# Cross-attention on one core: the key products A by eleven 64x64 block products instead of twelve, in a rewritten order of steps

## The chip, the cores and the metric

The kernel runs on one core of a Trainium2 chip, as one program. The metric is the device time of one execution in microseconds (us); the time before is the median of three executions. The engines are TensorE (PE; its weight loads are PEld), VectorE (DVE), ScalarE (ACT), GpSimd (POOL) and SyncE (SP, which issues transfers).

## The reference

Cross-attention of 16 batches, 256 queries of 256 features against 77 keys of 192 features, 8 heads of width 256, with a residual and a layer norm. The mask that is given is all ones.

```python
Q = (x @ Wq).reshape(B, -1, H, D).transpose(0, 2, 1, 3)      # x: 16 x 256 x 256
K = (ctx @ Wk).reshape(B, -1, H, D).transpose(0, 2, 1, 3)    # ctx: 16 x 77 x 192
V = (ctx @ Wv).reshape(B, -1, H, D).transpose(0, 2, 1, 3)
score = einsum('bhqd,bhkd->bhqk', Q, K) / sqrt(D)            # H = 8, D = 256
attn = softmax(where(mask, score, -inf), axis=-1)
o = einsum('bhqk,bhkd->bqhd', attn, V).reshape(B, -1, H * D)
out = o @ Wo + x
out = (out - mean(out)) * rsqrt(var(out) + 1e-5) * gamma + beta
```

All is float32.

## The kernel before

**What is computed.** Weights are multiplied first: G = Wq Wk^T / 16 for each head (tile `gA` holds the first 128 of ctx's 192 features, `gB` the last 64), and U = Wv Wo (`uA`, `uB`). Then A = G^T ctx^T for each head gives "keys" that x meets directly: scores = x A. A is made for a group of four batches at a time, `prepare_a`, into the tile `a`: for a pair of heads, 128-row products by `gA` (L193) and 64-row products by `gB` (L205), both in tiles of 32 output rows, 308 columns (4 batches x 77 keys); group 3 is made two batches at a time for its last pairs. ctx U ("values" that already passed Wo) comes from `prepare_vw` (L227 and L238), tile `vw`. 

**One batch** has two tiles of 128 queries. For each tile: `scores` (L303, PE), `shift` (L320, DVE: adds the mask's bias and finds each row's maximum), `exponential` (L340, ACT, eight instructions, one a head), a reciprocal (L355, DVE) and `weigh` (L361, POOL: multiplies by the reciprocal), `turn` (L371, DVE: transposes into `pT`). Then attention times values is done for both tiles together by `seven(b)` (L450, PE: seven block products instead of eight), which needs `sums(b)` (L431 to L434, POOL: sums of blocks of pT) and `differences(b)` (L414, POOL: sums of blocks of vw, tile `ts`). `add_seven(b)` puts the products together: `add_product` on DVE (L498: x plus the products in PSUM) and five additions on POOL (L484). Last the layer norm of each tile: `finish` (L506 and L509, DVE: statistics), `spread` (L527 and L528, ACT: logarithm and exponential that give the reciprocal deviation `rstd`), `normalise` (L548 and L577, DVE), and a transfer out.

**Order.** Nothing is planned by a scheduler: each engine runs its instructions in the order in which the program's text issues them, and waits on semaphores. The text is one loop over b from -1 to 14 whose body does the scores of batch b+1, its softmax, `seven(b)`, and the layer norm of batch b-1; every second body also makes the values of two batches and two pairs of heads of a coming A. A batch pair (a turn) is thus one body with that work and one without. Results of matmuls go through eight PSUM banks, given out in rotation (tag "mm"): a product that takes a bank waits until what was in it eight allocations ago has been read. ACT's copies (L963) empty the banks of vw and A. The work ahead of the loop (transposes, G, U, group 0 of A, the first softmax) is the prologue.

## Time and profile before

| | |
|---|---|
| median of 3 executions | 270.27 us (270.22 to 270.64) |
| the profiled execution | 269.95 us |
| its span in the trace | 268.2 us |
| granted clock of TensorE | 1.0 |
| busy PE / DVE / ACT / POOL | 262.5 / 185.9 / 157.6 / 173.2 us |

Busy times are sums over the span. A row of the timeline gives start, length, engine, line, operation, output and inputs, shape and how many in a row; a group's row gives count, total busy time and the mean of one in ns, then the idle time in front of it and what ended that. The engine's idle time counts only where the chain that ends last passes through it. The granted clock is 1.0 when TensorE runs at its full rate.

### The profile page before, as it was taken

How to read it: one execution, taken by the hardware profiler on the slowest of the kernel's cores; microseconds unless marked ns; L12 is line 12 of the kernel's file. 1: busy time of each engine (PE TensorE's matmuls, PEld its weight loads, DVE VectorE, ACT ScalarE, POOL GpSimd, SP SyncE). 2: the span in 40 equal slices, each digit the busy share in tenths (PEclk: the TensorE clock that was granted, in tenths of full speed). 3: DMA queues.
4: the chain of work that ended last, by engine and by line, in shares of the span. 5: the costliest groups of instructions: out<-in, count | busy, mean ns of one | idle time of the engine just before them, and what ended most of it. 6: DMA issues, size and time to landing. Idle time of an engine off the chain costs nothing.

```text
span 268.2 us, 14455 instructions
## 1 busy us (share of the span) xinstructions
PE 262.5 (98%) x6090; PEld 191.8 (72%) x6090; DVE 185.9 (69%) x808; ACT 157.6 (59%) x667; POOL 173.2 (65%) x240
## 2 busy tenths in 40 slices
PE   8999999999999999999999999999999999999992
PEld 8566578944984699459944995499669957985662
DVE  1555967493583868665886379647977887799785
ACT  3243336536857565955596468737775595636772
POOL 1042005728399739994799669965998799585452
PEclk9999999999999999999999999999999999999999
DMA  6989987901500130232012401340034010100112
GB/s 190 217 199 228 334 138 142 311 21 34 129 7 2 46 80 2 63 111 71 5 43 90 112 5 43 91 113 2 6 120 122 4 45 2 44 22 22 46 40 80
DMA packets 41696, 22.69 MB, mean 85 GB/s; under 512 B 24144, under 2 KB 40608, under 8 KB 41632
## 3 DMA queue, kind: packets, MB, share of 16 engines
q1 hardware_dynamic: 41248, 20.98, 30.1%
q0 software_dynamic: 384, 0.79, 1.3%
q8 instruction: 48, 0.79, 1.3%
q14 instruction: 16, 0.13, 0.2%
HBM read 17.57 MB, written 4.19 MB: 81 GB/s over the span
## 4 chain that ended last, share of the span: by engine, by line
PE 98%; DVE 1%; issue 0%; DVEq 0%
PE ps L303 25%; PE pa L193 13%; PE pv L227 11%; PE po L450 11%; PE pm L450 8%; PE pa L205 6%; PE pv L238 6%; PE po L383 4%; PE pu L773 3%; PE pr L263 2%; PE pgb L834 2%; PE pw L787 1%; PE idle L703 1%; PE pr L274 1%; PE phb L850 1%; PE po L399 1%
## 5 line engine op out<-in xcount | busy, mean ns | idle before, releaser
L340 ACT ACTIVATE s<-s,top 128x77 f32<-128x77 f32 x256 | 85.3, 346 | 44.2 <-DVE top L320 37.9
L303 PE MATMUL ps<-a,xT 128*32 128x154 f32 x2048 | 69.9, 294 | 0.0
L303 PEld LDWEIGHTS ps<-a,xT 128*32 128x32 f32 x2048 | 66.2, 110 | 1.2 <-issue 0.4
L361 POOL TENSOR_TENSOR p<-s,rden 128x512 f32<-128x512 f32 x64 | 47.5, 768 | 29.5 <-DVE rden L355 29.4
L320 DVE CUSTOM_DVE_ANT_0 s<-ps,bias 128x77 f32<-128x77 f32 x256 | 43.5, 232 | 14.3 <-PE ps L303 14.3
L340 ACT ACTIVATION_READ_ACCUMULATOR s<-s,top 128x1 f32 x224 | 42.0, 187 | 0.0
L193 PE MATMUL pa<-cA,gA 128*32 128x308 f32 (+1 forms) x576 | 36.6, 395 | 0.0
L193 PEld LDWEIGHTS pa<-cA,gA 128*32 128x32 f32 x576 | 18.3, 110 | 21.0 <-issue 7.0
L484 POOL TENSOR_TENSOR xg<-xg,m 128x256 f32<-128x256 f32 x39 | 28.7, 736 | 6.6 <-DVE xg L498 4.5
L577 DVE SCALAR_TENSOR_TENSOR xg<-xg,rstd,bet 128x256 f32<-128x256 f32 x27 | 22.9, 847 | 14.0 <-ACT rstd L528 12.6
L227 PE MATMUL pv<-uA,cA 128*32 128x512 f32 x256 | 30.6, 595 | 0.0
L371 DVE STREAM_TRANSPOSE pT<-p 128x640 f32<-128x640 f32 x32 | 25.5, 821 | 3.4 <-POOL p L361 3.3
L414 POOL TENSOR_TENSOR ts<-vw 128x768 f32<-128x768 f32 x13 | 24.0, 1848 | 5.9 <-ACT vw L963 5.9
L963 ACT COPY vw<-pv 128x512 f32<-128x512 f32 x32 | 17.8, 584 | 14.8 <-PE pv L227 8.3
L498 DVE TENSOR_TENSOR xg<-po,xg 128x256 f32<-128x256 f32 x31 | 11.5, 405 | 13.8 <-PE po L450 13.3
L320 DVE DVE_READ_ACCUMULATOR2_ANT top<- 128x1 f32 x256 | 20.8, 81 | 0.0
L205 PE MATMUL pa<-cB,gB 64*32 64x308 f32 (+2 forms) x512 | 20.4, 387 | 0.0
L963 ACT COPY a<-pa 128x308 f32<-128x308 f32 (+1 forms) x56 | 18.9, 395 | 1.9 <-PE pa L193 0.4
L205 PEld LDWEIGHTS pa<-cB,gB 64*32 64x32 f32 (+1 forms) x512 | 11.0, 110 | 11.4 <-issue 6.2
L548 DVE SCALAR_TENSOR_TENSOR xg<-xg,mv,gam 128x256 f32<-128x256 f32 x30 | 17.6, 588 | 0.1
L238 PE MATMUL pv<-uB,cB 64*32 64x512 f32 x256 | 17.3, 597 | 0.0
L227 PEld LDWEIGHTS pv<-uA,cA 128*32 128x32 f32 x256 | 7.5, 109 | 12.8 <-issue 9.9
(119 smaller groups left out, 404.1 us busy)
## 6 DMA issues: line engine op xcount, KB each, us to landing
xg<-in_x_dram SPq DMA_DIRECT2D x8, 512.0 KB, 4.4
xT<-in_x_dram SPq DMA_DIRECT2D x56, 64.0 KB, 2.6
out_dram<-xg SPq DMA_DIRECT2D x11, 256.0 KB, 2.2
wo<-in_L_xattn_Wo_dram SPq DMA_DIRECT2D x4, 512.0 KB, 7.8
wq_blk<-in_L_xattn_Wq_dram SPq DMA_DIRECT2D x12, 128.0 KB, 4.3
out_dram<-xg SPq DMA_DIRECT2D x10, 128.0 KB, 1.9
wk_blk<-in_L_xattn_Wk_dram SPq DMA_DIRECT2D x12, 96.0 KB, 3.6
wvT<-in_L_xattn_Wv_dram POOLq DMA_DIRECT2D x8, 96.0 KB, 6.6
```

Of the source, the lines that this page charges most:

```text
L193: nc.tensor.matmul(flat(o[i * BK : (i + 1) * BK]), gA[:, h, cols(dc, i)], flat(cA[:, batches, :]), start=not rest_first and n in opening, ...
L205: nc.tensor.matmul(flat(banks[j + k][i * BK : (i + wide) * BK]), gB[half(k), h // 2, dc * P + i * BK : dc * P + (i + wide) * BK], flat(cB[ ...
L227: nc.tensor.matmul(pv[k][i * BK : (i + 1) * BK], cA[:, b, k * BK : (k + 1) * BK], uA[:, parts, :, i], start=not rest_first, stop=rest_first,)
L238: nc.tensor.matmul(pv[k][i * BK : (i + 1) * BK], cB[half(k), b, k * BK : (k + 1) * BK], uB[half(k), parts, :, i], start=rest_first, stop=n ...
L303: nc.tensor.matmul(ps[m // 2][i * BK : (i + 1) * BK, m % 2 * 2 * S2 : (m % 2 + 1) * 2 * S2], xT_of[t // PT][:, j * NM + m, dc], flat(a_of[ ...
L320: nc.vector.tensor_tensor_reduce(s[:, h], ps[a][:, k * S2 : (k + 1) * S2], bias[:, b, :], scale=-1.0, scalar=FAR, op0=ALU.add, op1=ALU.min ...
L340: nc.scalar.activation(s[:, h], s[:, h], AF.Exp, bias=top[:, one], scale=-1.0, accum_out=den[:, one] if summed_by_act(t) else None,)
L361: nc.gpsimd.tensor_tensor(part, e_mh[:, :, :, keys], rden_mh.unsqueeze(3).to_broadcast(list(part.shape)), ALU.mult,)
L371: nc.vector.transpose(pT_of[t].rearrange("p n m q -> p m n q"), p.rearrange("p m (n k) -> p m n k", k=BK),)
L450: nc.tensor.matmul(out[i * BK : (i + 1) * BK], weight[:, i], moving, start=first and n == 0, stop=final and n == len(terms) - 1,)
L484: nc.gpsimd.tensor_tensor(to, to, what, ALU.add)
L963: nc.scalar.copy(dst, src)
```

## The change

**A by blocks.** For groups 1 to 3 and as long as b < 10, A of a pair of heads is made by `prepare_fast` instead of `prepare_a`. Each head's product is cut into blocks: eight block products of the first 128 features are replaced by seven (sums of blocks of G, tile `gS` and `gC`, times sums of blocks of ctx, tiles `cT` and `cD`), and four of the last 64 features stay, eleven in all. All are tiles of 64x64 with 154 columns (two batches x 77). Per pair of heads there are 44 matmuls (L360 in the kernel after). Two of a pair's 154-column results are copied by ACT (L369), and DVE puts the rest together with four additions a head (L372), each reading one PSUM bank and `a`. The sums of blocks are formed once in the prologue on POOL, with a few copies on ACT (`sums_of_g`, `last_sums_of_g`, `sums_of_c`, `differences_of_c`); `gA` is laid out by halves of the features for them.

**Statistics.** For the tiles of batches 0 to 9, `finish` takes the mean and the variance by two ACT activations that accumulate (L681, L682) instead of two DVE instructions.

**Order.** The loop's first ten bodies are replaced by pairs of a `long_step` (with the values and two pairs of A) and a `short_step`; the old body, a little simplified, does the rest. The layer norm of a batch comes later than before.

The core of the diff:

```diff
+        def products():
...
+            for pair in pairs():
...
+                for i in range(2):
+                    for ((bank, n), weight, moving), (start, stop, _) in zip(pair, flags):
+                        nc.tensor.matmul(
+                            bank[half(i), n],
+                            weight(i),
+                            moving,
+                            start=start,
+                            stop=stop,
+                        )
+                for ((bank, n), _, _), (_, _, one) in zip(pair, flags):
+                    if one:
+                        nc.scalar.copy(blocks[lone[id(bank)]][:, 0], by_batch(bank)[:, n])
...
+        def put_together(e):
+            mid, end, of = by_batch(mids[e]), by_batch(ends[e]), blocks[e]
+            plus(of[:, 3], mid[:, 2], of[:, 0])
+            plus(of[:, 1:3], mid[:, 0:2], of[:, 3:4].to_broadcast([P, 2, HB, S2]))
+            plus(of[:, 3], mid[:, 0], of[:, 2])
+            plus(of[:, 0:3], end, of[:, 0:3])
...
+        if by_act(t):
+            junk = st.tile([P, DI], F32, tag="junk", name=f"junk_{t}", bufs=1)
+            mean, var = (mv_of[g][:, j, n : n + 1] for n in range(2))
+            nc.scalar.activation(junk, y, AF.Identity, scale=1.0 / DI, accum_out=mean)
+            nc.scalar.activation(junk, y, AF.Square, bias=mean, scale=-1.0, accum_out=var)
+            return
         bn = st.tile([P, 6], F32, tag="bn", name=f"bn_{t}")
         nc.vector.bn_stats(bn, y)
...
+        turn_rest_last()
+        sums_of_c(1, 2)
         sum_of(uB)
         for t in range(QT):
             exponential(t)
             weigh(t)
+        differences_of_c(1, NG)
+        sums_of_c(2, NG)
...
+    def long_step(b):
...
+        statistics(tiles_of(b - 2))
+        works = work_of(b + 1) + work_of(b + 2)
+        for part_A, *_ in works:
+            part_A()
+        if now:
+            seven(b)
+        for _, part_B, _ in works:
+            part_B()
...
+            fasts.append(prepare_fast(g, n + k))
...
+        statistics(tiles_of(b - 1))
...
+        for t in tiles_of(b - 2):
+            normalise(t)
+        turn_some_x(g, n)
...
+        fasts[0][1](0)
+        fasts[0][1](1)
+        fasts[1][1](0)
+        behind.append(partial(fasts[1][1], 1))
+        for t in tiles_of(b - 1):
+            behind.append(partial(normalise, t))
...
+    def short_step(b):
...
+        seven(b)
+        weigh(new[0])
+        for _ in range(2):
+            if behind:
+                behind.pop(0)()
...
+        weigh(new[1])
+        turn(new[0])
+        while behind:
+            behind.pop(0)()
+        turn(new[1])
+        sums(b + 1)
+        add_seven(b)
...
+    ready = B - GB - GB // 2 - 1
+    for b in range(-1, ready, 2):
+        long_step(b)
+        short_step(b + 1)
+    statistics(tiles_of(ready - 2))
-    for b in range(-1, B - 1):
+    for b in range(ready, B - 1):
```

**POOL, the short step of a turn.** `ts` are the differences, `m` and `xg` the additions of `add_seven`, `ss` the sums, `pT` the turned tiles. Before:

```order
L414 TENSOR_TENSOR ts_1667<-vw_1378 128x768 [waits PE_49]
L484 TENSOR_TENSOR m_1735<-m_1735 128x128 [waits Activation_49]
L484 TENSOR_TENSOR m_1735<-m_1735 128x128 [waits Pool_49]
L484 TENSOR_TENSOR xg_518<-xg_518,m_1735 128x256 [waits DMAHW7_49,DVE_49]
L484 TENSOR_TENSOR xg_518<-xg_518,m_1735 128x2x128 [waits DVE_49,Pool_49]
L484 TENSOR_TENSOR xg_518<-xg_518,m_1735 128x256 [waits Pool_49]
L431 TENSOR_TENSOR ss_1750<-pT_1741 128x256
L432 TENSOR_TENSOR ss_1750<-pT_1741,pT_1739 128x256
L433 TENSOR_TENSOR ss_1750<-pT_1741,ss_1750 128x256 [waits Pool_49]
L434 TENSOR_TENSOR ss_1750<-pT_1739,ss_1750 128x256 [waits Pool_49]
```

After, the same step:

```order
L602 TENSOR_TENSOR ss_1838<-pT_1836 128x256 [waits DVE_49]
L603 TENSOR_TENSOR ss_1838<-pT_1836,pT_1831 128x256
L604 TENSOR_TENSOR ss_1838<-pT_1836,ss_1838 128x256 [waits Pool_49]
L605 TENSOR_TENSOR ss_1838<-pT_1831,ss_1838 128x256 [waits Pool_49]
L655 TENSOR_TENSOR m_1814<-m_1814 128x128 [waits Activation_49]
L655 TENSOR_TENSOR m_1814<-m_1814 128x128 [waits Pool_49]
L655 TENSOR_TENSOR xg_532<-xg_532,m_1814 128x256 [waits DMAHW7_49,DVE_49]
L655 TENSOR_TENSOR xg_532<-xg_532,m_1814 128x2x128 [waits DVE_49,Pool_49]
L655 TENSOR_TENSOR xg_532<-xg_532,m_1814 128x256 [waits Pool_49]
L532 TENSOR_TENSOR p_88<-s_1918,rden_2188 128x4x128 [waits DVE_49]
```

The four sums stand ahead of the five additions, the differences have gone to the long step, and the next long step's weighing (`p`) follows behind the additions.

**DVE, the short step, behind the shift.** `bn` and `mv` are statistics, `rden` the reciprocal, `xg` the rows that are normalised. Before:

```order
L506 BN_STATS bn_2482<-xg_831 128x6 [waits Pool_49]
L509 BN_AGGR mv_2484<-bn_2482 128x2 [waits DVE_49]
L355 RECIPROCAL rden_2486<-den_2473 128x8 [waits Activation_49]
L506 BN_STATS bn_2499<-xg_831 128x6 [waits Pool_49]
L509 BN_AGGR mv_2484<-bn_2499 128x2 [waits DVE_49]
L355 RECIPROCAL rden_2502<-den_2490 128x8 [waits Activation_49]
L548 SCALAR_TENSOR_TENSOR xg_831<-xg_831,mv_2484,gam 128x256
L577 SCALAR_TENSOR_TENSOR xg_831<-xg_831,rstd_2513,bet 128x256 [waits DVE_49,Activation_49]
L371 STREAM_TRANSPOSE pT_2655<-p_85 128x4x5x32 [waits Pool_49]
L371 STREAM_TRANSPOSE pT_2657<-p_86 128x4x5x32 [waits Pool_49]
```

After (`a` from `pf` are the additions that put A together):

```order
L526 RECIPROCAL rden_3026<-den_2940 128x8 [waits Activation_49]
L372 TENSOR_TENSOR a_2073<-pf_7_1_2734,a_2073 128x2x77
L372 TENSOR_TENSOR a_2073<-pf_7_1_2734,a_2073 128x4x77 [waits DVE_49]
L372 TENSOR_TENSOR a_2073<-pf_7_1_2734,a_2073 128x2x77 [waits DVE_49]
L372 TENSOR_TENSOR a_2073<-pf_7_1_2735,a_2073 128x6x77 [waits DVE_49]
L725 SCALAR_TENSOR_TENSOR xg_1033<-xg_1033,mv_2782,gam 128x256
L754 SCALAR_TENSOR_TENSOR xg_1033<-xg_1033,rstd_2790,bet 128x256 [waits DVE_49]
L526 RECIPROCAL rden_3036<-den_2949 128x8 [waits Activation_49]
L542 STREAM_TRANSPOSE pT_3040<-p_88 128x4x5x32 [waits Pool_49]
L725 SCALAR_TENSOR_TENSOR xg_1033<-xg_1033,mv_2782,gam 128x256
L754 SCALAR_TENSOR_TENSOR xg_1033<-xg_1033,rstd_2790,bet 128x256 [waits DVE_49]
L542 STREAM_TRANSPOSE pT_3045<-p_89 128x4x5x32 [waits Pool_49]
```

The statistics have left; the fourth head's additions and the normalisations of two tiles stand between the reciprocals and the turned tiles.

**ACT at batch 9**, where the paired steps end; `vw` and `a` are the copies that empty banks. Before:

```order
L340 ACTIVATE s_3537,den_3622<-s_3537,top_3538 128x77 [waits DVE_49,Pool_49]
L340 ACTIVATE s_3537,den_3622<-s_3537,top_3538 128x77 [waits DVE_49] x7
L963 COPY vw_3552<-pv_0_3553 128x4x128 [waits PE_49]
L963 COPY vw_3552<-pv_1_3554 128x4x128 [waits PE_49]
L963 COPY a_2988<-pa_4_0_0_3555 128x2x77 [waits PE_49]
L963 COPY a_2988<-pa_5_0_0_3556 128x2x77 [waits PE_49]
L963 COPY a_2988<-pa_4_0_0_3555 128x2x77
```

After:

```order
L511 ACTIVATE s_3740,den_3820<-s_3740,top_3741 128x77 [waits DVE_49,Pool_49]
L511 ACTIVATE s_3740,den_3820<-s_3740,top_3741 128x77 [waits DVE_49] x7
L681 ACTIVATE junk_3830,mv_3829<-xg_2223 128x256 [waits DMAHW6_49,Pool_49]
L682 ACTIVATE junk_3830,mv_3829<-xg_2223,mv_3829 128x256 [waits Activation_49]
L511 ACTIVATE s_3750,den_3837<-s_3750,top_3751 128x77 [waits DVE_49] x8
L681 ACTIVATE junk_3846,mv_3829<-xg_2223 128x256 [waits Activation_49,Pool_49]
L682 ACTIVATE junk_3846,mv_3829<-xg_2223,mv_3829 128x256 [waits Activation_49]
L1145 COPY vw_3767<-pv_0_3768 128x4x128 [waits PE_49]
L1145 COPY vw_3767<-pv_1_3769 128x4x128 [waits PE_49]
```

The statistics of two tiles, which wait for POOL, stand between the exponentials and ahead of the copies.

More of the change, by code (lines that the diff above doesn't have):

```diff
@@ L216, in prepare_a, with parts_of_g, sums_of_g @@
         return part_A, part_B, copies
+    add, subtract = (
+        partial(nc.gpsimd.tensor_tensor, op=op) for op in (ALU.add, ALU.subtract)
+    )
+    def parts_of_g():
+        parts = gA.rearrange("p (u e) (dc i c) -> p dc e u i c", e=2, dc=2, c=BK)
+        sums = gS.rearrange("p n (u e) (i c) -> p n e u i c", e=2, c=BK)
+        return [(parts, sums, e, own, other) for e, own, other in ((0, high, low), (1, low, high))]
+    def sums_of_g():
+        for parts, sums, e, own, other in parts_of_g():
+            nc.scalar.copy(sums[own, 0, e], parts[other, 1, e])
+            nc.scalar.copy(gC[own], gB[other, :, P:])
+        for parts, sums, e, own, other in parts_of_g():
+            s1, s2, s3 = (sums[own, n, e] for n in range(3))
+            add(s1, s1, parts[own, 1, e])
+            subtract(s2, s1, parts[own, 0, e])
+            subtract(s3, parts[own, 0, e], parts[own, 1, e])
@@ L893 @@
             a_of_pairs(a, rest_first=True)
+        gS = const.tile([P, 3, H, P], F32, tag="gS", name="gS")
+        sums_of_g()
         load_x(0)
@@ L976, with tiles_of, statistics @@
     last = NT - 1
-    for b in range(-1, B - 1):
+    def tiles_of(b):
+        return range(b * QT, (b + 1) * QT) if b >= 0 else ()
+    def statistics(tiles):
+        for t in tiles:
+            finish(t)
+        if tiles:
+            spread(tiles[0], tiles[-1] + 1)
+            invert(tiles[0], tiles[-1] + 1)
+    def long_step(b):
+        now, new = tiles_of(b), tiles_of(b + 1)
+        g, n = (b + 1) // GB + 1, (b + 1) % GB
+        if now:
+            for t in new:
+                scores(t)
+            for t in new:
+                shift(t)
+            for t in new:
+                exponential(t)
+        for m in range(0, 2) if b < 0 else range(b + 2, min(b + 3, B // 2)):
+            turn_last(m)
+        statistics(tiles_of(b - 2))
+        works = work_of(b + 1) + work_of(b + 2)
+        for part_A, *_ in works:
+            part_A()
+        if now:
+            seven(b)
+        for _, part_B, _ in works:
+            part_B()
+        fasts = []
+        for k in range(2):
+            fasts.append(prepare_fast(g, n + k))
+            if k == 0:
+                copy_out(works[:1])
+            fasts[k][0]()
+            if k == 0:
+                copy_out(works[1:])
+        statistics(tiles_of(b - 1))
+        if now:
+            for t in new:
+                weigh(t)
+        for t in new:
+            turn(t)
+        if b < 0:
+            for t in range(QT, GT, 2):
+                transpose_x(t)
+            bias_of(GB, B)
+        sums(b + 1)
+        if now:
+            add_seven(b)
+        for k in range(2):
+            differences(b + 1 + k)
+        for t in tiles_of(b - 2):
+            normalise(t)
+        turn_some_x(g, n)
+        if g < NG:
+            load_x((g * GB + n) // 2)
+            for k in range(2):
+                load_xT(g * GT + (n + k) * QT, g * GT + (n + k + 1) * QT, after_pool=k == 0)
+        fasts[0][1](0)
[4 more added lines that the diff above has]
+            behind.append(partial(normalise, t))
@@ new lines, in short_step @@
+    def short_step(b):
+        new = tiles_of(b + 1)
+        for t in new:
+            scores(t)
+        for t in new:
+            shift(t)
+        for t in new:
+            exponential(t)
+        seven(b)
[3 more added lines that the diff above has]
+                behind.pop(0)()
+        for m in range(b + 2, min(b + 3, B // 2)):
+            turn_last(m)
+        weigh(new[1])
[3 more added lines that the diff above has]
+        turn(new[1])
+        sums(b + 1)
+        add_seven(b)
@@ L980 @@
         new = range((b + 1) * QT, (b + 2) * QT)
-        for t in new if b >= 0 else ():
+        for t in new:
             scores(t)
-        for t in new if b >= 0 else ():
+        for t in new:
             shift(t)
@@ L991 @@
             load_x((g * GB + n) // 2)
-        for m in range(0, 2) if b < 0 else range(b + 2, min(b + 3, B // 2)):
-            turn_last(m)
         alone = b + 1 >= B - GB // 2
-        works = work_of(b + 1) if alone or n % 2 == 0 else []
-        for part_A, _, _ in works:
+        ahead = not alone and n % 2 == 0
+        works = work_of(b + 1) if alone or ahead else []
+        for part_A, *_ in works:
             part_A()
@@ L1017 @@
             break
-        for i, t in enumerate(new if b >= 0 else ()):
+        for i, t in enumerate(new):
             exponential(t)
-            if old:
-                finish(old[i])
+            finish(old[i])
             weigh(t)
-        ahead = works and not alone
-        if old and not ahead:
-            spread(old[0], old[-1] + 1)
         if ahead:
             copy_out(works)
-            if old:
-                spread(old[0], old[-1] + 1)
+        spread(old[0], old[-1] + 1)
+        if ahead:
             works = work_of(b + 2, rest_first=True)
@@ L1032 @@
                 part_B()
-            for part_A, _, _ in works:
+            for part_A, *_ in works:
                 part_A()
@@ L1040 @@
         if b < NS:
-            if now:
-                seven(b)
-            if old:
-                invert(old[0], old[-1] + 1)
-                normalise(old[0])
+            seven(b)
+            invert(old[0], old[-1] + 1)
+            normalise(old[0])
             for t in new:
                 turn(t)
-            if b < 0:
-                for t in range(QT, GT, 2):
-                    transpose_x(t)
-                bias_of(GB, B)
             if alone or ahead:
```

127 lines of the change are left out of this document (114 added, 13 removed).

## The prediction

> **What bounds the kernel now.** I read the page's busy line and chain first, then each engine's share in stretches of two batches, then the order of instructions inside one such stretch.
>
> ```profile
> PE 262.5 (98%) x6090; PEld 191.8 (72%) x6090; DVE 185.9 (69%) x808; ACT 157.6 (59%) x667; POOL 173.2 (65%) x240
> PE 98%; DVE 1%; issue 0%; DVEq 0%
> POOL 1042005728399739994799669965998799585452
> ```
>
> TensorE is busy for 98% of the span, and 98% of the chain that ended last is TensorE: every other engine's work is hidden today. (The third line is POOL's busy tenths in 40 slices of 6.7 us.) The stretches (columns: start and end, length, then busy time and instructions of PE, its weight loads, DVE, ACT, POOL, the granted clock, the DMA share) say how well:
>
> ```profile
> 50.00:55.40 5.40, 5.40 (x48) 4.67 (x50) 2.20 (x5) 2.12 (x10) 5.32 (x7) 1.00 0.75 248
> 55.40:61.27 5.87, 5.87 (x104) 2.41 (x104) 5.76 (x10) 1.60 (x5) 0.00 (x0) 1.00 0.01 3
> 134.95:162.83 27.88, 27.88 (x708) 20.22 (x704) 19.10 (x96) 18.18 (x84) 22.53 (x30) 1.00 0.21 60
> ```
>
> The third stretch is one turn of the steady state, two batches in 27.88 us, with the granted clock at 1.00. TensorE has no gap. POOL has 22.5 of 27.9, DVE 19.1, ACT 18.2: slack of 5, 9 and 10 us in sum, which says nothing yet of chains that run through several of them. The second row shows POOL wholly idle for 5.87 us before the first turn. TensorE's own pieces in a turn (start, length, operation; the next row's start is the true end):
>
> ```profile
> 80.72 2.26 PE L193 MATMUL pa<-cA,gA 128*32 128x308 f32 x32
> 82.91 1.09 PE L238 MATMUL pv<-uB,cB 64*32 64x512 f32 x16
> 83.79 1.24 PE L205 MATMUL pa<-cB,gB 64*32 64x308 f32 x32
> 84.83 1.06 PE L238 MATMUL pv<-uB,cB 64*32 64x512 f32 x16
> ...
> 88.60 2.26 PE L193 MATMUL pa<-cA,gA 128*32 128x308 f32 x32
> 90.67 0.62 PE L450 MATMUL pm<-vw,pT 128*32 128x128 f32 x16
> ...
> 94.59 4.37 PE L303 MATMUL ps<-a,xT 128*32 128x154 f32 x128
> 98.78 0.62 PE L450 MATMUL pm<-vw,pT 128*32 128x128 f32 x16
> ```
>
> **1. TensorE's saving.** For A, a turn holds two pairs of heads. A pair costs 2.07 us in L193 (88.60 to 90.67) and 1.04 in L205 (83.79 to 84.83), so two cost 6.22. Where L193 is followed by a tile of another height it takes 2.19 (80.72 to 82.91), so a change of tile shape costs 0.12; today a turn has two, 0.24. The new products have 64x64 tiles, as large in cells as 128x32, and 154 columns like the scores: 128 records in 4.19 us (94.59 to 98.78), 32.7 ns each. Two pairs take 2 x 88 records (the trace shows two per matmul written), 5.76 us, and three changes of shape, 0.36. That is 6.12 against 6.46, -0.34 a turn. Five turns: -1.7. The bounds come from the 64x64 rows of the prologue:
>
> ```profile
> 19.30 1.10 PE L850 MATMUL phb<-qT,kT_all 64*64 64x128 f32 x32
> 20.23 1.91 PE L834 MATMUL pgb<-qT,kT_all 64*64 64x256 f32 x32
> 21.95 1.22 PE L205 MATMUL pa<-cB,gB 64*64 64x308 f32 x16
> L773 PEld LDWEIGHTS pu<-wo,wv_turned 64*64 64x64 f32 x128 | 5.2, 133 | 2.0 <-PE pa L193 0.5
> ```
>
> 256 columns take 53.8 ns a record (1.72 us for 32), so 154 take 32.3, and the saving is 2.1. If four loads in parallel at 133 ns each set the pace (33.3), it is 1.2. I keep 32.7, the row with the same number of columns.
>
> The Trainium skill, "TensorE: Matmul & The Clock Gate", section "LDWEIGHTS (loading the stationary operand)", has a rule that speaks against this change: a load takes as long as its columns, columns/1.2 in ns. By it a 64-column load takes 53 ns; if they came one by one, 176 would take 9.4 us, 3.6 more than in my sum, and with five turns of that and nothing else late the time would be near 287. The row L850 does not bear it out: 32 loads and 32 matmuls of 128 columns pass in 0.93 us, 29 ns a pair. It stays as a rival below.
>
> **2. POOL's new prologue.** Sums of gA's blocks and of ctx's blocks are formed on POOL: before the sum for uB 8 operations of 154 columns, behind the first weighing one of 462 and 8 of 308. Prices:
>
> ```profile
> 50.11 1.27 POOL L902 TENSOR_TENSOR uB<-uB 128x512 f32<-128x512 f32 x1
> ...
> 52.69 2.71 POOL L361 TENSOR_TENSOR p<-s,rden 128x512 f32<-128x512 f32 x4
> 61.27 1.83 POOL L414 TENSOR_TENSOR ts<-vw 128x768 f32<-128x768 f32 x1 [5.88 <-ACT vw L963]
> ...
> 65.36 0.73 POOL L431 TENSOR_TENSOR ss<-pT 128x256 f32<-128x256 f32 x1
> ...
> 67.68 0.73 POOL L434 TENSOR_TENSOR ss<-pT,ss 128x256 f32<-128x256 f32 x1
> 71.77 1.06 PE L450 MATMUL pm<-ts,ss 128*32 128x128 f32 x32
> ```
>
> Two-input operations run at about 2.5 to 2.9 ns a column (1.27 for 512, 0.73 for 256); I give the copies 0.3 for 154 and 0.45 for 308. That makes 3.4 + 1.2 + 5.4 = 10.0 us behind 50.1. Of these 5.9 fall in the idle stretch. The first product with ts starts at 71.77 now, at 71.4 with the shorter first stage. POOL's queue ahead of ts is 50.1 + 3.4 (ctx sums) + 2.6 (uB) + 2.7 (weigh) + 6.6 + 2.2 (bias) + 3.05 (sums of batch 0) + 1.83 (ts) = 72.5. So TensorE waits +1.2 (0 if copies and broadcast sums are cheaper by a tenth, 2.5 if dearer by as much). The new sums of gA, some 10 us of POOL, lie before 50.1; there POOL's first seven slices have 12 of 70 tenths, so I count nothing for them; ACT's few new copies go the same way.
>
> **3. A ring through DVE and POOL.** DVE gets four additions a head, of 154, 308, 154 and 462 columns, each with one operand in PSUM and each dependent on the one before. Rows for that, and for everything else that DVE does in a turn:
>
> ```profile
> L498 DVE TENSOR_TENSOR xg<-po,xg 128x256 f32<-128x256 f32 x31 | 11.5, 405 | 13.8 <-PE po L450 13.3 <-PE po L383 0.5
> L516 DVE TENSOR_TENSOR xg<-po,xg 128x128 f32<-128x128 f32 x2 | 0.6, 286 | 0.0
> 108.05 0.23 DVE L320 CUSTOM_DVE_ANT_0 s<-ps,bias 128x77 f32<-128x77 f32 x1
> 108.21 0.55 DVE L548 SCALAR_TENSOR_TENSOR xg<-xg,mv,gam 128x256 f32<-128x256 f32 x1
> 108.79 0.84 DVE L577 SCALAR_TENSOR_TENSOR xg<-xg,rstd,bet 128x256 f32<-128x256 f32 x1
> ...
> 115.35 1.56 DVE L371 STREAM_TRANSPOSE pT<-p 128x640 f32<-128x640 f32 x2
> 116.83 1.26 DVE L165 STREAM_TRANSPOSE xT<-xT 128x512 f32<-128x512 f32 x2
> ...
> 122.72 0.76 DVE L498 TENSOR_TENSOR xg<-po,xg 128x256 f32<-128x256 f32 x2 [3.38 <-PE po L450]
> ...
> 130.39 0.48 DVE L577 SCALAR_TENSOR_TENSOR xg<-xg,rstd,bet 128x256 f32<-128x256 f32 x1
> L506 DVE BATCH_NORM_STATS2 bn<-xg 128x6 f32<-128x256 f32 x31 | 12.3, 396 | 0.1
> L509 DVE BATCH_NORM_AGGREGATE mv<-bn 128x2 f32<-128x6 f32 x31 | 5.6, 182 | 1.1
> 77.41 0.99 POOL L484 TENSOR_TENSOR m<-m 128x128 f32<-128x128 f32 x2
> 78.36 2.36 POOL L484 TENSOR_TENSOR xg<-xg,m 128x256 f32<-128x256 f32 x3
> ```
>
> 405 for 256 columns and 286 for 128 make 0.93 ns a column and 167 fixed: 0.31 + 0.45 + 0.31 + 0.60 = 1.67, with releases 1.7 a head, 6.8 a turn. Against it go four tiles' statistics (0.40 and 0.18, some 0.6 each) to ACT, so DVE stands at 19.1 + 6.8 - 2.4 = 23.5 of 27.5. ACT gains four statistics (rows in part 4) of 1.15 each and loses copies: below 23. In sums all fits. But POOL's order in the short step is turned: the four sums of batch b+1, which need DVE's last turned tile pT, now stand ahead of the additions for batch b, and these ahead of the next long step's weighing. So from one long step's pT to the next runs a closed chain, each member in its engine's order. DVE: additions to x 0.76, two normalisations at 1.2 (1.34 at 108.21 where POOL works beside it, 0.94 at 130.39 where it doesn't), xT 1.26, three heads 5.1, shift 16 x 0.16 = 2.6, reciprocal 0.17, the fourth head 1.7, a normalisation 1.2, reciprocal, pT 0.8, a normalisation 1.2, pT 0.8: 18.2, plus vr's 0.6 (one transpose of 512 columns, as in xT's pair) in the early turns and about 0.5 of waiting for TensorE's last head and the first exponentials. POOL: sums 3.05, additions 3.35, two weighings 2.7: 9.1. DVE's pT 0.8 closes it. Together 28.6 to 29.2, against TensorE's 27.54: +1.1 to +1.7 a turn, on the three turns from batch 3 to 9 (before batch 3 nothing is normalised): I take +4.0, near the upper end, because ACT adds to the same lateness. Its exponentials start late with the shift, statistics (2.3 for two tiles, and a logarithm and an exponential) stand behind them and ahead of the vw copies, and the first A of a turn waits for the second vw's bank. Bounds: at 0.94 a normalisation and 1.5 a head the ring is 26.9 and costs 0; at 1.34 and 1.9 it is 30 or a little more, +7.
>
> The Trainium skill, "GPSIMD Engine Reference", section "1. Specifications", says that POOL shares SBUF interfaces with VectorE and contends with DVE instructions that have two SBUF inputs. The trace agrees for L577, 0.48 with POOL idle and 0.84 beside it; the additions for A have one input in PSUM, and the page names no contention for those.
>
> **4. The changeover at batch 9.** Here ACT's row has the first tile's statistics, which wait for POOL's additions of batch 8, between the two tiles' exponentials, ahead of the copies that free banks for the next product. The row of the same place before, and what a statistic is made of (two activations of 256 columns and two reads of an accumulator):
>
> ```profile
> 197.50 0.59 ACT L963 COPY vw<-pv 128x512 f32<-128x512 f32 x1 [0.17 <-PE pv L227]
> L340 ACT ACTIVATION_READ_ACCUMULATOR s<-s,top 128x1 f32 x224 | 42.0, 187 | 0.0
> L842 ACT ACTIVATE gA<-pgb 128x256 f32<-128x256 f32 x6 | 2.0, 381 | 6.5 <-PE pgb L834 6.5
> ```
>
> The second vw copy waited for TensorE by only 0.17 us, so ACT was barely ahead. A statistic is 2 x (0.38 + 0.19) = 1.15; two stand in front now, 2.3 less that slack, and the wait for POOL may add the ring's lateness of a turn, 1.5: +2.0 (0 if POOL and ACT are early, 3.7).
>
> **5. Batches 10 and 11.** DVE leaves the turns late and must still normalise; before, TensorE never waited there. +1.0 (0 to 3).
>
> What is off the path: the 64x308 and 154-column lone copies on ACT replace longer ones; transfers keep their count, and the DMA share is 0.21 in a turn.
>
> **Sum**: -1.7 + 1.2 + 4.0 + 2.0 + 1.0 = +6.5. The profiled execution took 269.95 us (span 268.2 and 1.75 around it), so 276.45; the median shown is 0.3 above it: **276.8**.
>
> **Rivals.** (a) The covers hold, on the other side: the ring's place is DVE between two turned tiles; at normalisations of 0.94 and heads of 1.5 (pipelined, 0.38 for 256 columns as in the row at 122.72) it is below 27.54 and POOL catches up with ts. Then only -1.7 remains, with 0.0 to 0.6 lost at batch 9, on the profiled time or on the median: 268.25 to 269.2. For it: the sums of every engine leave 4 us. Against: ring and statistics are both serial. It decides once the ring is 1.1 us shorter: 0.2 less a normalisation and 0.1 less a head. (b) The ring just closes, prologue and changeover are paid: 269.95 - 1.7 + 1.2 + 2.0 + 0.5, with 0.3 for the median, is 272.3. (c) Weight loads set TensorE's pace: at 133 ns a load and two at a time, one for each half of the rows, 176 take 11.7 us instead of 5.76, 30 more over five turns, 298 with nothing else late; L850's 29 ns is against it. (The page cited in part 1 would have such a bound, at its own figure.) (d) DVE and POOL slow each other throughout (every normalisation 1.34, the weighings 1.7 instead of 1.38): 284 and more.
>
> **How the numbers follow.** My forecast (271 to 283 by itself) 0.47, (a) 0.24, (b) 0.18, (c) 0.03, (d) 0.08. The range from (a)'s lower end to the forecast's upper end, 268.2 to 283, leaves out (c), (d) and a little of (a). A difference of 0.2% (0.5 us) is about what a measurement can tell from none. Faster is (a) but for its upper part: 0.21; same 0.04; slower 0.75.
>
> **What would show it.** Right: L360's 88 records in 2.9 us, 5.8 a turn; gaps on TensorE ahead of the first L360 or scores of the turns from batch 3, released by ACT or DVE; ts of batch 0 late; DVE's L372 near 0.42 mean; ACT's L681 waiting for POOL at batch 9. Wrong: TensorE without gaps and turns of 27.5 (a); TensorE busy yet L360 near 5 us a pair (c); DVE idle in front of exponentials in each turn (the ring is slack).

## The result and the profile after

The change makes the kernel slower: 278.22 us (median of 4 executions, 277.78 to 278.28) against 270.25 (270.15 to 270.64) beside it, a ratio of 1.0289 with the interval 1.0271 to 1.0307. The forecast was 276.8. The profiled execution took 277.78 us with a span of 275.9, against 269.95 and 268.2.

The page after, its line of busy times, its line of the chain that ended last, and the granted clock in 40 slices:

```profile
PE 264.7 (96%) x6330; PEld 205.4 (74%) x6330; DVE 204.3 (74%) x848; ACT 172.1 (62%) x734; POOL 189.2 (69%) x264
PE 53%; DVE 19%; POOL 17%; ACT 5%; issue 3%; DMA 1%; SPq 0%; POOLq 0%; DVEq 0%; ACTq 0%
PEclk9999999999999999999999999999988999999998
```

The share of TensorE in the chain fell from 98% to 53%, while its busy share fell by two points only: a chain of DVE, POOL and ACT now sets the pace in places. Busy shares did not show that; the chain did. It does not say how much time is lost: in the ring experiment below TensorE has 43% of the chain, and the kernel is 5.3 us faster. Where the chain costs time is seen by cutting the span at the first scores of each long step. The stretches of the kernel before, its first short step, its changeover at batch 9 and all that follows (columns as in the prediction; each of its four turns takes 27.88 or 27.89):

```profile
66.71:74.81 8.10, 8.10 (x260) 7.76 (x256) 4.41 (x36) 6.63 (x35) 3.46 (x6) 1.00 0.47 114
...
186.34:203.08 16.74, 16.74 (x457) 12.41 (x453) 14.59 (x53) 10.39 (x48) 16.27 (x21) 1.00 0.21 60
203.08:268.20 65.12, 60.23 (x1568) 46.03 (x1559) 52.48 (x251) 39.23 (x170) 43.88 (x61) 1.00 0.14 41
```

The same stretches after, with the four turns between:

```profile
66.40:75.54 9.14, 8.34 (x260) 7.70 (x260) 7.40 (x44) 6.06 (x33) 8.98 (x11) 1.00 0.03 8
75.54:103.13 27.59, 27.59 (x760) 22.69 (x756) 20.03 (x97) 17.89 (x84) 20.84 (x30) 1.00 0.24 60
103.13:131.14 28.01, 27.79 (x757) 22.73 (x753) 22.70 (x102) 18.84 (x87) 21.21 (x29) 1.00 0.20 55
131.14:160.68 29.54, 28.86 (x767) 23.01 (x759) 24.20 (x104) 20.26 (x95) 21.42 (x29) 1.00 0.21 57
160.68:189.31 28.63, 28.28 (x761) 23.93 (x755) 22.72 (x101) 19.95 (x93) 21.09 (x30) 1.00 0.21 57
189.31:210.83 21.52, 18.50 (x457) 13.89 (x453) 15.07 (x57) 17.05 (x78) 14.54 (x21) 0.92 0.26 72
210.83:275.90 65.07, 60.21 (x1568) 45.23 (x1559) 50.92 (x249) 40.85 (x178) 44.75 (x62) 0.98 0.13 40
```

The first turn is what the change would give alone: 27.59, 0.29 less than before, with no gap on TensorE. From there: first stage -0.31 (first scores at 66.40 instead of 66.71), first short step +1.04, the four turns -0.29, +0.13, +1.65, +0.75, the changeover +4.78, the rest -0.05. Sum +7.7, the difference of the spans. Over half of the loss is in one place, the changeover.

In the turns, the ring that the prediction drew shows in these rows: POOL's sums, which wait for DVE's last turned tile of a short step, POOL's weighing in the next long step, and two waits of TensorE for DVE (start, length, operation; in brackets the idle time ahead and what ended it):

```profile
136.07 0.74 POOL L602 TENSOR_TENSOR ss<-pT 128x256 f32<-128x256 f32 x1 [1.13 <-DVE pT L542]
142.35 2.71 POOL L532 TENSOR_TENSOR p<-s,rden 128x512 f32<-128x512 f32 x4
...
146.73 0.31 PE L360 MATMUL pf<-cA,gA 64*64 64x154 f32 x1 [0.45 <-DVE xg L669]
161.40 2.82 PE L468 MATMUL ps<-a,xT 128*32 128x154 f32 x80 [0.25 <-DVE a L372]
```

POOL waits for DVE's turned tile and then works without a pause up to the weighing, for which DVE's next turned tiles wait. TensorE waits for a bank that DVE's additions empty (L669) and for DVE's additions that put A together (L372). These two waits make 0.7 of the 3.41 us by which the three turns exceed 27.59. The rest lies in products that pass more slowly without a wait this long: the 176 of L360 take 7.07 us here, from 145.06 to 152.13, and 5.93 in the first turn.

Rows of the changeover, POOL's, ACT's and TensorE's:

```profile
198.19 2.65 POOL L655 TENSOR_TENSOR xg<-xg,m 128x256 f32<-128x256 f32 x3
200.00 0.42 ACT L681 ACTIVATE junk<-xg 128x256 f32<-128x256 f32 x1 [2.17 <-POOL xg L655]
201.19 1.23 PE L202 MATMUL pa<-cA,gA 128*32 128x154 f32 x32
205.44 1.08 PE L621 MATMUL pm<-vw,pT 128*32 128x128 f32 x16 [3.02 <-ACT vw L1145]
```

POOL's additions for batch 8 come late, and ACT stands 2.17 us for them ahead of its first statistic. Behind that are still the second tile's exponentials and its statistic, and only then the copies of vw, for which TensorE stands 3.02 us. The windows of TensorE's product behind the gap show a second loss (the granted clock is the third number from the end):

```profile
205.44:208.65 3.21, 3.21 (x64) 2.98 (x68) 1.56 (x2) 3.18 (x13) 2.11 (x3) 0.53 0.17 58
208.65:210.83 2.18, 2.18 (x73) 1.80 (x69) 2.18 (x5) 0.71 (x2) 1.21 (x2) 1.00 0.51 118
```

Over these 3.21 us the granted clock is 0.53 on average (the two eights in the line of 40 slices; the last section shows what the average is made of). `seven(9)` takes 5.39 us in the two windows.

### The profile page after: what moved, and what is told of

It is laid out like the page before. It is cut to its first block, busy times and chain, and to the rows that moved or that the text cites. A ratio compares the mean times of both kernels' runs of the same rounds, so it can differ in the third digit from the quotient of the medians.

```text
span 275.9 us, 15101 instructions
## 1 busy us (share of the span) xinstructions
PE 264.7 (96%) x6330; PEld 205.4 (74%) x6330; DVE 204.3 (74%) x848; ACT 172.1 (62%) x734; POOL 189.2 (69%) x264
## 4 chain that ended last, share of the span: by engine, by line
PE 53%; DVE 19%; POOL 17%; ACT 5%; issue 3%; DMA 1%; SPq 0%; POOLq 0%; DVEq 0%; ACTq 0%
PE ps L468 12%; PE po L621 6%; DVE a L372 5%; PE pv L392 5%; PE pm L621 5%; PE po L554 4%; ACT s L511 4%; PE pa L202 4%; PE pf L360 3%; DVE s L485 3%; POOL p L532 3%; POOL xg L655 3%; PE pv L403 3%; PE pu L950 3%; DVE pT L542 2%
## 5 line engine op out<-in xcount | busy, mean ns | idle before, releaser
L468 PEld LDWEIGHTS ps<-a,xT 128*32 128x32 f32 x2048 | 65.4, 110 | 3.6 <-issue 1.8
L532 POOL TENSOR_TENSOR p<-s,rden 128x512 f32<-128x512 f32 x64 | 45.6, 736 | 32.2 <-DVE rden L526 32.1
L485 DVE CUSTOM_DVE_ANT_0 s<-ps,bias 128x77 f32<-128x77 f32 x256 | 42.3, 233 | 1.8 <-PE ps L468 1.7
L372 DVE TENSOR_TENSOR a<-pf,a 128x154 f32<-128x154 f32 x80 | 33.8, 433 | 4.4 <-PE pf L360 2.0
L526 DVE RECIPROCAL rden<-den 128x8 f32<-128x8 f32 x32 | 6.3, 198 | 22.9 <-ACT s L511 22.7
L754 DVE SCALAR_TENSOR_TENSOR xg<-xg,rstd,bet 128x256 f32<-128x256 f32 x27 | 18.0, 668 | 6.6 <-ACT rstd L705 5.2
L392 PEld LDWEIGHTS pv<-uA,cA 128*32 128x32 f32 x256 | 9.1, 110 | 12.6 <-issue 8.5
L602 POOL TENSOR_TENSOR ss<-pT 128x256 f32<-128x256 f32 x13 | 9.7, 746 | 11.4 <-DVE pT L542 10.4
L360 PE MATMUL pf<-cT,gS 64*64 64x154 f32 x240 | 17.4, 290 | 0.0
L621 PE MATMUL po<-vr,pT 128*32 128x256 f32 x208 | 16.9, 379 | 0.2 <-issue 0.2
L621 PE MATMUL pm<-ts,ss 128*32 128x128 f32 x416 | 15.0, 281 | 1.0 <-POOL ts L585 0.8
```

The source lines that it names most:

```text
L360: nc.tensor.matmul(bank[half(i), n], weight(i), moving, start=start, stop=stop,)
L372: nc.vector.tensor_tensor(out, *of, ALU.add)
L392: nc.tensor.matmul(pv[k][i * BK : (i + 1) * BK], cA[:, b, k * BK : (k + 1) * BK], uA[:, parts, :, i], start=not rest_first, stop=rest_first,)
L468: nc.tensor.matmul(ps[m // 2][i * BK : (i + 1) * BK, m % 2 * 2 * S2 : (m % 2 + 1) * 2 * S2], xT_of[t // PT][:, j * NM + m, dc], flat(a_of[ ...
L485: nc.vector.tensor_tensor_reduce(s[:, h], ps[a][:, k * S2 : (k + 1) * S2], bias[:, b, :], scale=-1.0, scalar=FAR, op0=ALU.add, op1=ALU.min ...
L532: nc.gpsimd.tensor_tensor(part, e_mh[:, :, :, keys], rden_mh.unsqueeze(3).to_broadcast(list(part.shape)), ALU.mult,)
```

## The experiments

Each is the changed kernel with the edits named, timed against the kernel before on the same chip (before: 270.36 to 270.60 in these runs).

### One part undone at a time

**The statistics at batch 9 behind the copies.**

```diff
-            finish(old[i])
+            if not ahead:
+                finish(old[i])
...
         if ahead:
             copy_out(works)
+            for t in old:
+                finish(t)
```

> At batch 9 the two tiles' statistics on ScalarE are issued behind the copies of vw and A instead of between the exponentials. Theory (changeover): ScalarE no longer waits 2.2 us for POOL's additions of batch 8 ahead of the copies, so TensorE's 3.1 us gap ahead of seven(9) closes and the clock stays at 1.0 behind it, which saves another 1.5: 278.2 - 4.6 = 273.6 (273 to 274.3). Rival (the lateness is that of the whole ring: DVE and POOL are late anyway and TensorE waits at the next place): at most 1.5 us gained, 276.7 or more.

275.67 us, ratio 1.0187 (1.0167 to 1.0206). In the changeover all of the theory holds: it takes 17.22 us (189.92 to 207.14) instead of 21.52, -4.30, without a gap ahead of `seven(9)` and without a fall of the clock. But the time fell by 2.55 only, since what follows got longer: 66.76 instead of 65.07 us. One row shows a new wait, 0.93 of these 1.69 us, in batch 11:

```profile
222.53 0.99 PE L202 MATMUL pa<-cA,gA 128*32 128x154 f32 x24 [0.93 <-DVE xg L669]
```

That fits a lateness of DVE which the stall had hidden: while TensorE stood, DVE caught up, and with the stall gone it is paid later. That is the prediction's part 5.

**The gap filled.** TensorE repeats the last products of A three times where it stood still; the repeats add into the same banks, so A of those heads is not the right one here.

```diff
...
-            for part_A, *_ in works:
-                part_A()
+            for k, (part_A, *_) in enumerate(works):
+                part_A(4) if k and b == ready else part_A()
```

> At batch 9 TensorE repeats the last 32-column products by gA three times (96 records, 1.05 us each time), accumulating into the same banks, in what is now its 3.1 us gap; A of two heads' pairs for two batches is thereby wrong. All waits stay. Theory (clock): seven(9) runs slowly, 3.2 us instead of 1.75 for its first four products, because the granted clock fell to 0.5 after the idle time; with TensorE busy it runs at full rate: 276.6 to 276.9, 1.4 to 1.6 less. Rival (the products are slow because their operands come late): 278.2, no change, or more.

`seven(9)` now runs at the full clock, in one window:

```profile
206.50:210.41 3.91, 3.91 (x136) 3.57 (x128) 2.39 (x4) 3.67 (x14) 2.00 (x3) 1.00 0.22 64
```

3.91 us instead of 5.39: 1.48 us of the changeover is the fallen clock and not the wait itself. The time, 277.92 us (277.84 to 278.35), is not clear of the changed kernel's (277.78 to 278.28), and the expected 276.6 to 276.9 was missed. In the profiled execution the changeover began 1.04 us later (0.86 of that before the first scores, which the edit doesn't touch), and 66.0 us followed it instead of 65.07. That the clock was the cause is shown by the rows; by the time it would have stayed open.

**The ring.** Two normalisations on DVE go, within the long step, from behind the turned tiles to between the reciprocals, and ACT's statistics of the same batch go from the long step to behind the exponentials of the short step ahead of it.

```diff
-        statistics(tiles_of(b - 2))
...
-            for t in new:
-                weigh(t)
+            weigh(new[0])
+            for t in tiles_of(b - 2):
+                normalise(t)
+            weigh(new[1])
...
-        for t in tiles_of(b - 2):
-            normalise(t)
...
         seven(b)
+        statistics(tiles_of(b - 1))
         weigh(new[0])
...
-    statistics(tiles_of(ready - 2))
```

> The statistics of the batch two back go from ScalarE's place behind the long step's exponentials to its idle time at the end of the short step before, and that batch's two normalisations on DVE from behind the turned tiles to between the two reciprocals of the long step, where DVE waited 2.5 us. Theory (ring): the chain from one long step's turned tile to the next loses 2.8 to 3.1 us, falls below TensorE's 27.55, and the turns 2 to 4 (28.0, 29.5, 28.6) take 27.6 each, 3.3 us less; the changeover at batch 9 becomes shorter by up to 2.5 as POOL arrives earlier: 272.5 to 275. Rival (DVE and POOL are simply too full, or contend): the turns stay above 28.3 and the time at 277 or more.

272.90 us, ratio 1.0090 (1.0066 to 1.0114), 5.3 us less than the changed kernel. The last turn, the changeover, and `seven(9)` by itself:

```profile
159.16:186.75 27.59, 27.59 (x761) 22.65 (x757) 23.15 (x103) 20.67 (x95) 21.55 (x29) 1.00 0.24 62
186.75:204.69 17.94, 16.93 (x456) 12.33 (x451) 11.59 (x48) 14.81 (x66) 12.57 (x17) 1.00 0.24 70
200.75:204.69 3.94, 3.94 (x128) 3.60 (x132) 2.29 (x3) 3.80 (x14) 2.13 (x3) 1.00 0.19 56
```

The turns take 27.59, 27.97, 27.97 and 27.59: 2.65 of the 3.41 us that the ring cost are back. And the changeover, in which no engine's order changed, falls from 21.52 to 17.94: its gap is 1.01 us instead of 3.02, and the clock stays at 1.00. What follows takes 66.15 us instead of 65.07, as in the first experiment. So most of the changeover's loss needed two things at once, the ring's lateness, which reaches ACT through DVE and POOL, and the statistics ahead of the copies: without either, most of it goes.

**POOL's sums of ctx for groups 2 and 3**, moved out of the prologue behind the long steps of b = 1 and 3.

```diff
-        sums_of_c(2, NG)
...
+        if b in (1, 3):
+            sums_of_c(2 + b // 2, 3 + b // 2)
```

> The sums of ctx's blocks for groups 2 and 3 go from POOL's queue ahead of batch 0's products to the ends of the long steps 1 and 3 (one group each, some 4 us). Theory: ts of batch 0 is ready in time, and the 0.8 us that TensorE waited at 72.5 goes; but 4 us of POOL now lie in the turns of the ring, where POOL idled 3.2 for the first reciprocal of the short step: 277.0 to 278.2. Rival (POOL's sums are in the ring's way): the ring grows by up to 1 to 3 us and the time goes above 278.5.

277.55 us, ratio 1.0254 (1.0232 to 1.0276). The wait for ts is gone: the first short step takes 8.13 us instead of 9.14. Of the 1.0 us, 0.6 returns in the third and fourth turn (58.79 us instead of 58.17), behind the two turns into which POOL's work was moved (it lies at 97 and at 126 us, in the first and second turn).

**The three together.**

> The edits of e1 (statistics behind the copies at batch 9), e3 (ring shortened) and e4 (sums of ctx later) together. Theory (three separate losses, and a DVE that is still late behind batch 9): 272.9 from e3, less 0.7 for ts, less 1.2 for the changeover (17.94 us from the scores of batch 9's step to the next, 16.75 before), plus about 0.6, since e1 showed that a shorter changeover leaves DVE later in batches 10 and 11 (66.8 us to the end instead of 65.1): 271.5 (270.7 to 272.3). Rival (the gains add up in full): 267.5 to 269.5. Rival (they are one and the same lateness): 272.9.

271.31 us (10 executions), ratio 1.0032 (1.0016 to 1.0047): 6.9 of the 8.0 us are accounted for by three edits that change only the order. The time is the expected one, but not by the expected terms: batches 10 and 11 did not get longer (65.4 us follow the changeover, 66.15 in the ring experiment), and instead the second and third turn took 28.40 and 28.85. In these turns this kernel differs from the ring experiment, which has 27.97 twice, by POOL's moved sums alone.

### Is it the place on DVE, or DVE's sum?

Four dummy operations of 128x384 are added to DVE in every second step, once in the short step, inside the ring that the prediction drew, and once in the long step between the reciprocals, outside it.

```diff
+    def pad():
+        for _ in range(4):
+            nc.vector.memset(junkd, 0.0)
...
-            for t in new:
-                weigh(t)
+            weigh(new[0])
+            pad()
+            weigh(new[1])
```

(This is the one outside. Inside, `pad()` stands instead in the short steps from b = 2 on, ahead of the second weighing, `weigh(new[1])`.)

> The changed kernel, and in each short step from batch 3's on (four of them) four memsets of a scratch tile on DVE, some 1.4 us, ahead of the second weighing: inside the ring. Theory (ring): each full turn grows by 1.4, from batch 3 to 9 three turns, and the lateness at batch 9 too: 278.2 + 4.2 to 5.6 = 282.4 to 283.8. Rival (TensorE or the sum of DVE's work bounds the turns, DVE being busy 74%): 278 to 279.5.

> The same four memsets, four times, but in the long steps between the two reciprocals, where DVE waited 2.5 us for exponentials. Theory (ring): hidden, 278.2 to 278.7. Rival (DVE's sum of work counts): as much as the same memsets inside the short step, 280 or more.

The ring's period is read between the same turned tile of successive long steps, the second `pT` there. In the changed kernel:

```profile
115.45 0.84 DVE L542 STREAM_TRANSPOSE pT<-p 128x640 f32<-128x640 f32 x1 [0.49 <-POOL p L532]
...
145.10 0.85 DVE L542 STREAM_TRANSPOSE pT<-p 128x640 f32<-128x640 f32 x1 [0.49 <-POOL p L532]
...
174.14 0.84 DVE L542 STREAM_TRANSPOSE pT<-p 128x640 f32<-128x640 f32 x1 [0.49 <-POOL p L532]
```

With the work inside:

```profile
118.31 0.85 DVE L542 STREAM_TRANSPOSE pT<-p 128x640 f32<-128x640 f32 x1 [0.49 <-POOL p L532]
...
149.92 0.84 DVE L542 STREAM_TRANSPOSE pT<-p 128x640 f32<-128x640 f32 x1 [0.49 <-POOL p L532]
...
180.90 0.85 DVE L542 STREAM_TRANSPOSE pT<-p 128x640 f32<-128x640 f32 x1 [0.49 <-POOL p L532]
```

With it outside:

```profile
116.73 0.84 DVE L542 STREAM_TRANSPOSE pT<-p 128x640 f32<-128x640 f32 x1 [0.49 <-POOL p L532]
...
146.38 0.84 DVE L542 STREAM_TRANSPOSE pT<-p 128x640 f32<-128x640 f32 x1 [0.49 <-POOL p L532]
...
175.45 0.84 DVE L542 STREAM_TRANSPOSE pT<-p 128x640 f32<-128x640 f32 x1 [0.50 <-POOL p L532]
```

The periods are 29.65 and 29.04 in the changed kernel, 31.61 and 30.98 inside, 29.65 and 29.07 outside. Inside the work adds 1.96 and 1.94 to the two periods, all of its own cost (16 operations, 6.0 us busy and 1.9 idle ahead of them: 1.98 for four). Outside it adds nothing to them: it lies in time in which DVE waited for ACT's exponentials. The second reciprocal of the long step, in the changed kernel and with the work outside:

```profile
112.90 0.20 DVE L526 RECIPROCAL rden<-den 128x8 f32<-128x8 f32 x1 [2.54 <-ACT s L511]
...
114.18 0.20 DVE L526 RECIPROCAL rden<-den 128x8 f32<-128x8 f32 x1 [0.56 <-ACT s L511]
```

DVE's busy sum is nearly the same in both (210.0 and 210.5 us), so it is the place. The times agree in kind: 286.99 us inside (ratio 1.0604, 1.0576 to 1.0631), 279.34 outside (1.0321, 1.0298 to 1.0344). The first is more than was expected, because four operations cost 1.98 and not 1.4, and the gap at the changeover grew to 3.70. The second is 1.1 above the changed kernel, and lies between the theory's 278.2 to 278.7 and the rival's 280. In its profiled execution 1.26 us of that lies before the first scores (67.66 instead of 66.40), ahead of the first of the added operations; the four turns together are 0.7 longer and the changeover 0.45 shorter. Why the first stretch varies is not settled, so the time alone would not decide; the periods do.

### Can the order be mended?

**Statistics of batches 8 and 9 back on DVE**, with the ring's and the sums' edits:

```diff
-        return fast(t // QT)
+        return t < NT - (GB + GB) * QT
```

> e3 and e4, and the statistics of batches 8 and 9 on DVE again, where it waits 3.6 us for the second exponentials of each of those steps, so that ScalarE's exponentials, copies and statistics no longer stand in one row behind POOL. Theory: changeover 16.75 as in the kernel before, 65.1 to 65.5 behind it, four turns of 27.6 to 28.0: span 267.8, time 269.2 to 269.9 against 270.3 of before, faster by 0.15 to 0.4%. Rival (ScalarE wasn't what was late there; DVE waits for POOL instead, and its shift with it): 271 or more.

271.49 us (12 executions), ratio 1.0037 (1.0025 to 1.0049). The changeover is as before the change, 16.73 us, and 65.35 follow. But the second and third turn take 28.41 and 28.82 us, with TensorE waiting among the first products of A:

```profile
PE pf L360 <- DVE xg L669: 1.6, 2, 1.0
```

(An answer of the trace on TensorE's waits: total, how often, the longest.) These products take banks that `add_product` (L669) empties, and that stands on DVE behind both turned tiles, and these wait for POOL's weighing. POOL's moved sums lie ahead of that. That they are a part of the cause is shown by the three edits together, where the same sums made the same turns longer (28.40 and 28.85 against 27.97), and by the kernels below, where moving them moves the loss.

**DVE's two additions between the two turned tiles of the long step**, in addition:

```diff
...
-        for t in new:
-            turn(t)
+        turn(new[0])
+        if now:
+            for t in now:
+                add_product(t)
+        turn(new[1])
...
```

> e8, and in the long steps DVE's two additions of seven(b) stand between the two turned tiles instead of behind them. In e8 the first A of the turns from batches 3 and 5 still waits 0.59 and 1.00 us for a bank that these additions read last. Theory: they come 0.85 us earlier, those waits shrink to 0 and 0.2, the turns of 28.4 and 28.8 to 27.8 and 28.0: 271.5 - 1.4 = 270.1 (269.5 to 270.6), the same as before within 0.2%. Rival (the second turned tile is then 0.64 later, POOL's sums with it, and the ring binds again): 271.5 or more.

269.80 us (9 executions), ratio 0.9969 (0.9953 to 0.9986), turns 27.59, 27.59, 28.21, 27.59. One turn still waits 0.4 us.

**POOL's sums one turn earlier** (behind b = -1 and 1), and in another kernel **the sums of group 3 one turn later** (behind b = 5 instead of 3):

> e9 with POOL's sums of ctx for groups 2 and 3 one turn earlier (behind the first and the second long step instead of the second and third). Theory: what POOL does late in the turns from batches 3 and 5 is what makes those additions late, and the first turn has room for it (no normalisations yet): 0.4 to 0.8 less than e9, 269.5 (269.0 to 270.0), 0.1 to 0.4% faster than before. Rival (3.5 us of POOL ahead of the first short step's weighing delay batch 1): the first turn of 27.59 grows by 1 or more, and the time is above e9's.

269.86 us (12 executions), ratio 0.9975 (0.9965 to 0.9985): inside the expected range, but no better than the kernel it was made from, so the expected gain of 0.4 to 0.8 is missing; the loss moved to the second turn, 28.32.

> e9, with POOL's sums of ctx for group 3 behind the long step of batch 5 instead of 3. Theory: in e9's profile only the turn from batch 3 (28.21 us) was longer than TensorE's 27.59, and its short step holds one of the last transposes of vr; the step behind the long step of batch 5 has none, 0.7 us less on DVE, and so has room for POOL's 3.5 us: all four turns 27.6, 269.8 - 0.6 = 269.2 (268.8 to 269.7). Rival (POOL's 3.5 us cost the same in any turn): 269.8, no change from e9.

269.36 us (6 executions, 268.78 to 269.55) against 270.39 beside it, ratio 0.9957 (0.9939 to 0.9974). The page's busy times and chain:

```profile
PE 261.2 (98%) x6330; PEld 204.2 (76%) x6330; DVE 210.1 (79%) x856; ACT 169.6 (64%) x718; POOL 191.0 (72%) x272
PE 96%; DMA 2%; DVE 1%; SPq 0%; issue 0%; DVEq 0%
```

All four turns take 27.59, the first short step 8.13, the changeover 16.77, and TensorE has 96% of the chain again. (Its share is no measure of the loss here either: the kernel with the sums one turn earlier is 0.5 us slower and has 54%.) DVE and POOL are busier than in the changed kernel (210.1 against 204.3, 191.0 against 189.2). This version beats the kernel before by about 1.0 us, and the changed one by 8.9. In the spans (267.0 against 268.2) nearly all of that lies in the four turns, 0.29 each, in which TensorE had no gap before; so it is the block products that gain it, once the other engines' order hides what they add. No run has the new order with the old products.

## Why the prediction was right, and where not

The mechanism held: slower, through a ring of DVE and POOL, a late ts and the changeover. That the sum came within 1.4 us is in part luck: one term was 2.8 us too small and three others 1.8 too large. By the terms of the sum:

1. **TensorE's saving, -1.7**: measured -0.31 in the first stage and -0.29 in each of four turns at the full pace, -1.5. The two pairs of the first stage by themselves:

```profile
60.48:66.40 5.92, 5.92 (x176) 5.70 (x176) 1.00 0.01 3
```

176 products in 5.92 us, 33.6 ns each: the 32.7 ns from the row of the scores nearly held, and the rival in which weight loads set the pace (11.7 us) did not.

2. **ts of batch 0, +1.2**: +1.0. The forecast for ts was 72.5; TensorE's first product with it, in the timeline:

```profile
72.47 1.08 PE L621 MATMUL pm<-ts,ss 128*32 128x128 f32 x32 [0.80 <-POOL ts L585]
```

3. **The ring, +4.0**: +3.4 (28.01, 29.54 and 28.63 against 27.59). Its period was 29.65 and 29.04, the forecast 28.6 to 29.2. One of the signs named for being wrong, DVE idle in front of exponentials in each turn, was there all the same (2.54 us ahead of the long step's second reciprocal): the ring was not slack, since in that stretch it ran through POOL. The heads of four additions (groups of L372; partitions x elements, count, busy time, mean ns, idle):

```profile
L372 DVE TENSOR_TENSOR a<-pf,a 128x462 f32<-128x462 f32 x20 | 12.8, 640 | 1.0
L372 DVE TENSOR_TENSOR a<-pf,a 128x154 f32<-128x154 f32 x40 | 12.3, 306 | 2.6 <-PE pf L360 2.0
L372 DVE TENSOR_TENSOR a<-pf,a 128x308 f32<-128x308 f32 x20 | 9.6, 479 | 0.7
```

Two of 306 ns, one of 479 and one of 640 make 1.73 us; the estimate was 1.67. Three heads in a row, 12 operations, take 5.42 us in the timeline, 1.8 a head where 1.7 was taken:

```profile
150.86 5.42 DVE L372 TENSOR_TENSOR a<-pf,a 128x154 f32<-128x154 f32 x12
```

One reading behind this term was wrong. The prediction took the normalisation at 130.39 of the kernel before (0.48 us) for one beside which POOL does not work. POOL weighs there:

```profile
128.95 3.16 POOL L361 TENSOR_TENSOR p<-s,rden 128x512 f32<-128x512 f32 x4 [3.36 <-DVE rden L355]
```

Where POOL is idle the same operation takes 0.48 too (at 242.63 and 256.01 in that trace), so the lower price stands; but beside this weighing it was not slowed, so not every POOL operation slows it.

The runs with dummy work show the ring by its period. What the ring experiment moved was two things at once, normalisations and ACT's statistics; no run parts them.

4. **The changeover, +2.0 with bounds 0 and 3.7**: +4.78, the term that was mis-sized, and outside its own bounds. ACT's wait for POOL and the four activations were there as described. Not in the sum was that the wait also cost TensorE its clock: 1.48 us by the run that filled the gap. 4.78 - 1.48 = 3.3 would have lain inside the bounds, near the upper one.

5. **Batches 10 and 11, +1.0**: -0.05. It was not wrong as a cause, but it doesn't add to term 4: the stall there gives DVE its time back. The run without the stall has the lateness, +1.69, with one wait of 0.93 for DVE. Terms 4 and 5 were summed as if independent; they cover each other.

So the forecast of 276.8 is 1.4 short of 278.22: term 4 is 2.8 too small, terms 2, 3 and 5 together 1.8 too large, term 1 gains 0.2 less than forecast: 1.2 together. Another 0.13 lies around the span (1.88 against 1.75), and 0.14 between the profiled execution and the median (0.44 where 0.3 was taken).

Of the rivals, "the covers hold" gave 268.25 to 269.2. It was wrong for this order and near for another: the mended kernel runs at 269.36. The prediction said that the ring needed to be 1.1 us shorter; in the order of the ring experiment two normalisations are taken out of it, and the last turn is at 27.59, though the two before it still take 27.97.

## What to carry to other kernels

Work that is given to an engine with slack in its sum is free only if it lies off every closed chain from one turn to the next: draw the chain, add it up, and compare it with the bound engine's turn. Where two such costs follow each other, ask what the first one's stall gives back before adding the second. And look at the order before giving up a change that saves little on the bound engine: here the same block products cost 8 us in one order and gained 1 in another.
